# Edge pieces in three buffers of two steps in a GNN-and-MoE kernel on one core

## The chip, the cores and the metric

The kernel runs on one NeuronCore of one Trainium2 chip. The metric is device time in microseconds, from the first to the last instruction of one launch and what the launch adds. The names of the engines are those of the profile: PE (matrix multiply, with PEld for its weight loads), DVE (vector), ACT (scalar, activations), POOL (GpSimd, which issues the indirect transfers) and SP (which issues most plain transfers). Each engine works through its own instructions in order.

## The reference, cut to what matters

There are 6250 nodes with 256 features and 100,000 edges with 96 features, sorted by their target node `dst`. A node needs the sum, the maximum and the mean over its edges; these go with the normalized node features through a two-layer network (1024 hidden units), and the result through a mixture of 16 experts of which two are chosen per node.

```python
out1 = segment_sum(edge_attr, col); cnt = segment_sum(ones, col)
out2 = where(cnt > 0, segment_max(edge_attr, col), 0)
out3 = out1 / maximum(cnt, 1.0)
h = concatenate([x, out1, out2, out3, u[batch]], axis=1)      # x is layer-normed
h = relu(h @ W1 + b1) @ W2 + b2                               # returns h + x
# then, on the layer-normed result: top-2 of 16 experts, relu MLP 256-512-256, layernorm, residual
```

All in float32.

## The kernel before, in words

**Tiles and groups.** The nodes are 50 tiles of P = 125 rows, in 13 groups (`GRP`) of GS = 4 tiles, the first of two; the groups run from the last nodes to the first. Groups 0 and 1 (GW = 2) gather their few edges directly: one indirect transfer brings a window of WE = 20 edges per node (`take_window`), and `cut_window`, `sum_window` and `max_window` reduce it. All other groups get their sums from the edge stream.

**The edge stream** (`steps`, `load_edges`, lines 177 to 323). The first 95,000 edges lie in seven regions of JR = 6, 5, 5, 10, 21, 20 and 28 steps; the regions run from the last edges to the first. A step holds one edge for each of 125 x 8 runs (partitions times RR = 8). From step to step DVE carries a running sum and a running maximum backwards through each run: four operations of 125 x 768 elements per step, L309 and L310 (the carried values, masked where a new node begins) and L312 and L313 (the new edges added and compared). In a region's first step ACT copies instead (L305, L306). The results, `rw`, hold 192 values for each edge and are stored to `rows_d` in DRAM (L322). When a region is done, `chain_runs` carries the values over runs and partitions (over PE, L394 to L420) and POOL stores them to `carry_d` (L430). A node's sums are then gathered from `rows_d` (`take_edges`, L712) and `carry_d` (`take_carry`, L719) and joined on DVE (`join_edges`, L725).

Steps come in pieces of up to JS = 3: `chunks` lists 34 of them. A piece has a tile `raw` (edges loaded) and a tile `rw` (rows to store), each from a pool of two buffers. After a piece's last DVE operation SP issues the load of the piece two further on, then the store of this one; both are issued in two halves (80 and 45 partitions). For region 0 the address of the store comes from a register (`rows_of`, `away`). The buffers of `raw` and `rw` also serve, before the stream starts, for the windows of groups 0 and 1 and for the node ids (`early`).

**The order of the work** is written by hand: `at_slot(T, fn, ...)` puts pieces of a group's work in slots, 12 per group, and within a slot the functions issue instructions to all engines. A cost is kept for DVE: what a slot has left goes to the edge stream (`next(stream)`), which thus lies between the other DVE operations in a fixed order. For a group whose hidden layer begins at slot B:

- `take_x` at B - 20 issues the load of x on SP (L666) into one of three buffers `xt`; `stats_x` at B - 14 and B - 13 reads it on DVE (L676).
- `turn`, `hidden` (L761, ACT L763) and `output` (L769) are the network on PE; `residual` (L774), `root_b` (L783, the store of x1 on SP), `scale_b` and `norm_b` (L797, ACT, at B + 15) follow, then `turn_b` (L806).
- `logits`, `choose` (L821 to L828), `rank` (L834 to L841, which makes `mm` and `M`), `rank_2` (L848 on PE), `place` (L857 to L870) find each row's place at its experts, and `send` (L874, POOL) scatters the rows to `xg_d`.

After the last group the experts run in 57 blocks (`run_block`, L1047 to L1066), and a last part adds their results, normalizes and writes the output (L1383 to L1421).

Of the kernel before, what the change touches and what calls it, by code (L numbers as in the profile page):

```python
# [9 lines left out]
F32 = mybir.dt.float32  # L10
# [9 lines left out]
P = 125  # L20
PA = 80
RR = 8
GW = 2
WE = 20
WB = 5
JR = (6, 5, 5, 10, 21, 20, 28)
GR = (1, 1, 1, 2, 3, 2, 1)
JS = 3
KB = 250
GS = 4  # L30
BT = (1, 2, 2, 3, 4) + 6 * (5,) + (4, 2, 2)
# [3 lines left out]
SLOTS = 12  # L35
SLOT = 4.6
IB = (1, 1, 1, 2, 3, 5)
# [5 lines left out]
def kernel(  # L43
# [45 lines left out]
    assert len(BT) % 2 == 0 and (NS - 1) // 4 - NA // 4 - 1 >= len(BT) // 2 and NA % 4  # L89
    assert NA <= -(-(2 * (N - P * GRP[-2][1]) - NE * (SB - 1)) // SB)  # L90
    assert KR == 32 and HC % 4 == 0 and GS * P <= 512 and NT <= GS * NE and wpack.shape[1] == WROW and D == DC * 128 and GF <= 128 and EF <= 128
    assert WE % (2 * WB) == 0 and WB * EF <= 512 and N0 == 2 and GW == 2 and WE <= RR * JS and P * GRP[GW - 1][0] <= EP * JR[0] <= ER // 2 and all(i == 1 for i in IB[:GW])

    dram = ctx.enter_context(tc.tile_pool(name="dram", bufs=1, space=DRAM))

# [70 lines left out]
    keep = [di_p.tile([P, RR, j], F32, name="keep%d" % c) for c, j in enumerate(JR)]  # L166
    bar = [di_p.tile([P, RR, j], F32, name="bar%d" % c) for c, j in enumerate(JR)]
    kall = di_p.tile([P, len(JR), RR], F32, name="kall")
    rawp = edges.enter_context(tc.tile_pool(name="raw", bufs=2, side="right"))
    chunks = []  # L170
    for c, j in enumerate(JR):
        k = -(-j // JS)
# [4 lines left out]
    def load_edges(i):  # L177
        c, s, n = chunks[i]
        e0, J = REG[c]
        raw = rawp.tile([P, RR, JS, EF], F32, name="raw")  # L180
        src = edge[e0:e0 + EP * J].rearrange("(p r j) f -> p r j f", p=P, j=J)
        for o, i_ in halves(raw[:, :, :n], src[:, :, s:s + n]):
            nc.sync.dma_start(o.rearrange("p r j f -> p r (j f)"), i_.rearrange("p r j f -> p r (j f)"))
        raws[i] = raw

    rwp = edges.enter_context(tc.tile_pool(name="rw", bufs=2, side="right"))
    ix = edges.enter_context(tc.tile_pool(name="ix", bufs=1, side="right"))
    chp = edges.enter_context(tc.tile_pool(name="ch", bufs=1, side="right"))
    banks = ctx.enter_context(ExitStack())
    eps = banks.enter_context(tc.tile_pool(name="eps", bufs=1, space=PSUM))  # L190

# [5 lines left out]
    gtp = mlp.enter_context(tc.tile_pool(name="gt", bufs=2))  # L197
    sm = mlp.enter_context(tc.tile_pool(name="sm", bufs=2))
    xrp = mlp.enter_context(tc.tile_pool(name="xr", bufs=1))
    pTp = banks.enter_context(tc.tile_pool(name="pT", bufs=1, space=PSUM))  # L200
    accp = banks.enter_context(tc.tile_pool(name="acc", bufs=5, space=PSUM))
    pGp = banks.enter_context(tc.tile_pool(name="pG", bufs=1, space=PSUM))
# [5 lines left out]
    nf = ix.tile([P, 1], F32, name="nf")  # L208
    misfit = ix.tile([1, 1], I32, name="misfit")
    shift = ix.tile([1, 1], I32, name="shift")  # L210
    early = rwp.tile([P, RR, JS, 2 * EF], F32, name="rw").rearrange("p r j f -> p (r j f)")
    L100 = E // 100
    ids100 = early[:100, 0:L100 + WE].bitcast(I32)
    viol = early[:100, L100 + WE:3 * L100 + WE].rearrange("p (h k) -> p h k", h=2)
# [77 lines left out]
    def steps():  # L292

        for i, (c, s, n) in enumerate(chunks):
            e0, J = REG[c]
            if s + n == J:
                mark_runs(c)
                yield 1.5, False, None
            raw, prev = raws.pop(i), prevs.pop(c, None)
            rw = rwp.tile([P, RR, JS, 2 * EF], F32, name="rw")  # L300
            bcast = [P, RR, EF]
            for j in reversed(range(n)):
                x_j, su, mx = raw[:, :, j, :], rw[:, :, j, 0:EF], rw[:, :, j, EF:]
                if prev is None:
                    nc.scalar.copy(su, x_j)  # L305
                    nc.scalar.copy(mx, x_j)  # L306
                    prev = x_j, x_j
                else:
                    nc.vector.tensor_tensor(su, prev[0], keep[c][:, :, s + j, None].to_broadcast(bcast), op=OP.mult)  # L309
                    nc.vector.tensor_tensor(mx, prev[1], bar[c][:, :, s + j, None].to_broadcast(bcast), op=OP.min)  # L310
                    yield 1.9, False, None
                    nc.vector.tensor_tensor(su, su, x_j, op=OP.add)  # L312
                    nc.vector.tensor_tensor(mx, mx, x_j, op=OP.max)  # L313
                    prev = su, mx
                    if j:
                        yield 1.9, True, None
            prevs[c] = prev
            if i + 2 < len(chunks):
                load_edges(i + 2)
            to = rows_of(c).rearrange("(p r j) f -> p r j f", p=P, j=J)  # L320
            for o, i_ in halves(to[:, :, s:s + n], rw[:, :, :n]):
                nc.sync.dma_start(o.rearrange("p r j f -> p r (j f)"), i_.rearrange("p r j f -> p r (j f)"))  # L322
            yield 1.9, True, c if s == 0 else None
# [224 lines left out]
    def take_window(g, i, w):  # L548
        j = GRP[g][0] - W0 + i
        nc.gpsimd.indirect_dma_start(out=w.rearrange("p k f -> p (k f)"), out_offset=None, in_=flat,  # L550
                                     in_offset=IndirectOffsetOnAxis(ap=win_i[:, j:j + 1], axis=0))
        G[g].setdefault("win", []).append(w)
# [525 lines left out]
    def at_slot(T, fn, *a, cost=0.0):  # L1078
        tasks.append((T, len(tasks), fn, a, cost))
# [21 lines left out]
    for g, (a, z) in enumerate(GRP):  # L1101
        B, n = SLOTS * g, z - a
        if g:
            if g > 1:
                at_slot(max(0, B - 20), take_x, g)
                at_slot(B - 14, stats_x, g, 0, cost=1.2)
                at_slot(B - 13, stats_x, g, 1, cost=1.2)
            if g > 1:
                at_slot(B - 11, root_x, g)
                at_slot(B - 10, scale_x, g, cost=0.5)  # L1110
            at_slot(B - 9, norm_x, g)
            for i in range(n):
                if g >= GW:
                    late = 3 if g == GW else 0
                    at_slot(B - 10 + late + i // 2, take_edges, region[g], g, i)
                    at_slot(B - 9 + late + i // 2, take_carry, region[g], g, i)
                else:
                    for h in range(2):
                        at_slot(2 * i + h, cut_window, g, i, h * WE // 2, (h + 1) * WE // 2, None)
                        at_slot(2 * i + 1 + h, sum_half, g, i, h)  # L1120
                    at_slot(2 * i + 1, max_window, g, i, cost=4.7)
                    at_slot(2 * i + 2, add_window, g, i, cost=0.9)
                    at_slot(2 * i + 2, mask_window, g, i, cost=0.4)
                    at_slot(min(2 * i + 5, SLOTS - 2), mean_window, g, i)
            at_slot(B - 7, keep_x, g)
            for k in range(DC):
                at_slot(B - 6 + k, turn, g, k)
            for i in range(n if g >= GW else 0):
                at_slot(B - (4 if g == GW else 6) + i // 2, join_edges, g, i, cost=0.6)
                at_slot(B - (4 if g == GW else 5) + i // 2, mask_edges, g, i)  # L1130
            for k in range(DC, KC + 1):
                at_slot(B - 3 + k - DC + (1 if g == GW and k < DC + 2 else 0), turn, g, k)
        for i in range(n):
            at_slot(B + HC + 1 + i, residual, g, i, cost=1.1)
        early = GS - n
        at_slot(B + SLOTS + 1 - early, root_b, g)
        at_slot(B + SLOTS + 2 - early, scale_b, g, cost=0.3)
        at_slot(B + SLOTS + 3, norm_b, g)
        for k in range(DC):
            at_slot(B + SLOTS + 4 + k, turn_b, g, k)  # L1140
        at_slot(B + SLOTS + 6, logits, g)
        at_slot(B + SLOTS + 7, choose, g, cost=2.2)
        at_slot(B + SLOTS + 8, rank, g, cost=1.3)
        at_slot(B + SLOTS + 9, rank_2, g)
        at_slot(B + SLOTS + 10, place, g, cost=1.5)
        for i in range(n):
            at_slot(B + SLOTS + 11 + i // 2, send, g, i)
# [38 lines left out]
                                fill[:, None, :].to_broadcast([128, NE, DR]))  # L1186

    at_slot(4, fill_rows)

    def loads_1():  # L1190
        take_x(0)
# [21 lines left out]
        nc.vector.tensor_add(c1, ps_u, b1c)  # L1213

    def windows_of(t, n):
        t = t.rearrange("p r j f -> p (r j f)")
        return [t[:, h * WE * EF:(h + 1) * WE * EF].rearrange("p (k f) -> p k f", f=EF) for h in range(n)]

    a, z = GRP[0]
# [1 line left out]
    base.append(chp.tile([P, RR, 2 * EF], F32, name="ct").rearrange("p r f -> p (r f)")[:, 0:(NT - W0) * 2 * EF]  # L1221
                .rearrange("p (t f) -> p t f", f=2 * EF))
    w1u = wk.tile([P, GS, D], F32, name="xn", bufs=1).rearrange("p i d -> p (i d)")[:GF, 0:HID]
    cut_x = windows_of(xrp.tile([P, GS, 2, DR], F32, name="xr"), 1)[0]
    cut_w = w2s[:P].rearrange("p k d -> p (k d)")[:, 0:WE * EF].rearrange("p (k f) -> p k f", f=EF)
    with tc.manual_schedule():
        load_all_ids()
# [60 lines left out]
    with tc.manual_schedule():  # L1288
# [4 lines left out]
        bounds(0)  # L1293
        index_windows(0)
        for i in range(z - a):
            take_window(0, i, windows_of(rawp.tile([P, RR, JS, EF], F32, name="raw"), 1)[0])
        root_x(0)
        counts(0)
        for t in reversed(range(a1, z1)):
# [3 lines left out]
        bounds(1)  # L1303
        index_windows(1)
        for h in range(2):
            for w in windows_of(rwp.tile([P, RR, JS, 2 * EF], F32, name="rw"), 2):
                take_window(1, len(G[1].get("win", [])), w)
        stats_x(1, 0)
        stats_x(1, 1)
# [20 lines left out]
        for k in range(DC, KC + 1):  # L1330
            turn(0, k)
        cuts += [cut_x]
        for i in range(2):
            load_edges(i)
        for c in range(1, len(JR)):
            load_ids(c)
# [137 lines left out]
```

## Time and profile before

| | us |
|---|---|
| median of 3 runs (lowest, highest) | 1442.02 (1439.64, 1451.39) |
| the profiled execution, its own time | 1443.29 |
| its span, first to last instruction | 1441.3 |
| PE busy | 1193.9 |
| DVE busy | 892.9 |
| ACT busy | 511.2 |
| POOL busy | 530.9 |
| DMA traffic over the span | 292.27 MB, mean 203 GB/s |

Busy time is the time in which an engine executes; the rest of the span it waits. Where the profile names a releaser of a wait, that is what came last by its semaphores. The stages of the execution: set-up and windows until about 125 us, edge stream beside groups until about 790 us, the last groups and the experts until about 1350 us, the last part until the end. PE's clock is granted by a throttle; 1.00 is full speed, and in this profile it is either 1.00 or 0.50. The DMA share is the mean busy share of the core's 16 DMA engines.

### The profile page before, as it was taken

How to read it: one execution, taken by the hardware profiler on the slowest of the kernel's cores; microseconds unless marked ns; L12 is line 12 of the kernel's file. 1: busy time of each engine (PE TensorE's matmuls, PEld its weight loads, DVE VectorE, ACT ScalarE, POOL GpSimd, SP SyncE). 2: the span in 40 equal slices, each digit the busy share in tenths (PEclk: the TensorE clock that was granted, in tenths of full speed). 3: DMA queues.
4: the chain of work that ended last, by engine and by line, in shares of the span. 5: the costliest groups of instructions: out<-in, count | busy, mean ns of one | idle time of the engine just before them, and what ended most of it. 6: DMA issues, size and time to landing. Idle time of an engine off the chain costs nothing. (4 is left out here: it accounts for less than half of the span.)

```text
span 1441.3 us, 16536 instructions
## 1 busy us (share of the span) xinstructions
PE 1193.9 (83%) x4835; PEld 833.1 (58%) x4835; DVE 892.9 (62%) x2319; ACT 511.2 (35%) x1178; POOL 530.9 (37%) x611
## 2 busy tenths in 40 slices
PE   2687377979668779898788999898999999999673
PEld 1353243645435354654455566787888888888562
DVE  5477587969766979878677332344444445444277
ACT  3484135554327353353324432321122212212133
POOL 4123043554574645354251622334333233233100
PEclk9898688989888989999898999999999999999897
DMA  5954758796778996986877323656677887666296
GB/s 167 202 150 125 202 144 229 205 244 184 217 186 239 253 256 173 272 226 179 239 213 225 87 79 102 198 174 230 214 245 248 273 266 240 214 228 226 88 273 195
DMA packets 156309, 292.27 MB, mean 203 GB/s; under 512 B 31379, under 2 KB 95652, under 8 KB 148910
## 3 DMA queue, kind: packets, MB, share of 16 engines
q1 hardware_dynamic: 119870, 234.35, 55.1%
q0 software_dynamic: 36224, 56.33, 13.7%
q8 instruction: 41, 0.67, 0.2%
q14 instruction: 62, 0.51, 0.1%
q10 hardware_dynamic: 112, 0.41, 0.1%
HBM read 169.70 MB, written 123.21 MB: 203 GB/s over the span
## 5 line engine op out<-in xcount | busy, mean ns | idle before, releaser
L761 PE MATMUL acc<-inT,w1x 128*128 128x500 f32 (+1 forms) x832 | 374.2, 600 | 0.0
L761 PEld LDWEIGHTS acc<-inT,w1x 128*128 128x128 f32 x832 | 162.6, 203 | 179.4 <-issue 177.3
L1066 POOL DMA_INDIRECT y_d<-yb,to_i x114 | 134.2, 1178 | 292.5 <-ACT yb L1065 269.8
L1047 PE MATMUL acc<-xT,wt 128*128 128x256 f32 x912 | 221.2, 385 | 7.8 <-ACT hb L1053 6.2
L1060 PE MATMUL acc<-wt,hb 128*128 128x256 f32 x912 | 207.8, 380 | 7.0 <-DVE hb L1051 7.0
L874 POOL DMA_INDIRECT xg_d<-xr,pos_i x100 | 130.0, 1300 | 224.0 <-DVE xr L870 144.0
L769 PE MATMUL acc<-w2s,hT 128*125 128x256 f32 x800 | 190.0, 395 | 11.5 <-ACT hT L763 11.5
L1060 PEld LDWEIGHTS acc<-wt,hb 128*128 128x128 f32 x912 | 172.5, 190 | 32.9 <-DVE hb L1051 9.4
L1047 PEld LDWEIGHTS acc<-xT,wt 128*128 128x128 f32 x912 | 168.1, 190 | 39.2 <-ACT hb L1053 15.7
L769 PEld LDWEIGHTS acc<-w2s,hT 128*125 128x125 f32 x800 | 155.2, 198 | 36.5 <-ACT hT L763 11.9
L1065 ACT ACTIVATE yb<-yb,xb 128x256 f32<-128x256 f32 x114 | 51.7, 500 | 347.5 <-issue 294.3
L763 ACT ACTIVATE hT<-acc,c 128x500 f32<-128x500 f32 (+1 forms) x104 | 68.4, 658 | 208.5 <-PE acc L761 206.3
L1063 DVE TENSOR_TENSOR yb<-acc,xb 128x512 f32<-128x512 f32 x57 | 39.4, 691 | 163.1 <-PE acc L1060 163.1
L309 DVE TENSOR_TENSOR rw<-rw,keep 125x768 f32<-125x768 f32 x81 | 76.8, 948 | 85.1 <-DMA rows_d<-rw 78.0
L485 POOL DMA_INDIRECT gb<-in_dst_dram,blk_i x50 | 69.2, 1383 | 115.8 <-DVE blk_i L482 54.2
L312 DVE TENSOR_TENSOR rw<-rw,raw 125x768 f32<-125x768 f32 x88 | 85.7, 973 | 0.0
L1027 DVE COPY xT<-pT 128x512 f32<-128x512 f32 x57 | 39.3, 690 | 74.3 <-PE pT L1025 74.1
L313 DVE TENSOR_TENSOR rw<-rw,raw 125x768 f32<-125x768 f32 x88 | 83.7, 951 | 0.0
L719 POOL DMA_INDIRECT cg<-carry_d,next_i x44 | 70.2, 1595 | 36.4 <-DMA carry_d<-ct 18.0
L310 DVE TENSOR_TENSOR rw<-rw,bar 125x768 f32<-125x768 f32 x81 | 79.5, 981 | 0.0
L712 POOL DMA_INDIRECT at<-rows_d,first_i x44 | 60.5, 1374 | 34.6 <-PE acc L761 13.6
L806 PE MATMUL pT<-ident,xr 125*128 125x125 f32 x100 | 23.3, 320 | 53.8 <-ACT xr L797 44.6
(294 smaller groups left out, 1525.4 us busy)
## 6 DMA issues: line engine op xcount, KB each, us to landing
wt<-in_wpack_dram SPq DMA_DIRECT2D x57, 1026.0 KB
rows_d<-rw SPq DMA_DIRECT2D x27, 1440.0 KB
rows_d<-rw SPq DMA_DIRECT2D x27, 810.0 KB
raw<-in_edge_dram SPq DMA_DIRECT2D x27, 720.0 KB
xb<-xg_d SPq DMA_DIRECT2D x57, 258.0 KB
raw<-in_edge_dram SPq DMA_DIRECT2D x27, 405.0 KB
eb<-in_eb_dram SPq DMA_DIRECT2D x57, 128.0 KB
rows_d<-rw SPq DMA_DIRECT2D x7, 960.0 KB
```

Of the source, the lines that this page charges most:

```text
L309: nc.vector.tensor_tensor(su, prev[0], keep[c][:, :, s + j, None].to_broadcast(bcast), op=OP.mult)
L310: nc.vector.tensor_tensor(mx, prev[1], bar[c][:, :, s + j, None].to_broadcast(bcast), op=OP.min)
L312: nc.vector.tensor_tensor(su, su, x_j, op=OP.add)
L313: nc.vector.tensor_tensor(mx, mx, x_j, op=OP.max)
L485: nc.gpsimd.indirect_dma_start(out=gbs_[t], out_offset=None, in_=dst_b, in_offset=IndirectOffsetOnAxis(ap=blk_i[:, t:t + 1], axis=0))
L719: nc.gpsimd.indirect_dma_start(out=cg, out_offset=None, in_=carry_d[0:EP * (c + 1), :], in_offset=IndirectOffsetOnAxis(ap=next_i[:, t:t + ...
L761: nc.tensor.matmul(pH[:, :n * P], w1x[:, k, ms], inT[:, k, :n * P], start=False, stop=(k == KC - 1))
L769: nc.tensor.matmul(pO, G[g]["hT"][m][:, i * P:(i + 1) * P], w2s[:, m, :], start=(m == 0), stop=(m == HC - 1))
L874: d = nc.gpsimd.indirect_dma_start(out=xg_d[:, :], out_offset=IndirectOffsetOnAxis(ap=G[g]["pos"][:, i, k:k + 1], axis=0), in_=G[g]["xr"][ ...
L1047: nc.tensor.matmul(pB[i][:, half, :], wt[:, k * FF + m * 128:k * FF + (m + 1) * 128], xT[:, k, :], start=(k == 0), stop=(k == DC - 1))
L1060: nc.tensor.matmul(pY[:, h, :], hb[:, m, h * 128:(h + 1) * 128], wt[:, W2O + m * D:W2O + (m + 1) * D], start=(m == order[0]), stop=(m == o ...
L1066: d = nc.gpsimd.indirect_dma_start(out=y_d[:, :], out_offset=IndirectOffsetOnAxis(ap=BL[b]["to"][:, h:h + 1], axis=0), in_=yb[:, h, :], in ...
```

## The change

Pieces have at most two steps instead of three (`JS`), and `raw` and `rw` have three buffers each instead of two (`JB`); the load issued after a piece is that of the third piece on. The memory of `raw` and `rw` stays as it was (six steps each). Since a buffer of two steps is too small for a window pair, the windows and the node ids get pools of their own, `win0` and `win1`, which are closed before `raw` and `rw` are opened: `open_raw` just before the first loads, `open_rows` in slot 9. `raw` moves to the other side of the memory. And `take_x` of a group is three slots later, at B - 17. The order of the instructions on PE, DVE, ACT and POOL stays the same; on SP there are 49 pieces with four transfers each instead of 34, and the loads of x stand later among them.

```diff
-JS = 3
+JS = 2
+JB = 3
...
-    rawp = edges.enter_context(tc.tile_pool(name="raw", bufs=2, side="right"))
...
-        raw = rawp.tile([P, RR, JS, EF], F32, name="raw")
+        raw = EP_["raw"].tile([P, RR, JS, EF], F32, name="raw")
...
-    rwp = edges.enter_context(tc.tile_pool(name="rw", bufs=2, side="right"))
...
+    win1 = ExitStack()
+    w1p = win1.enter_context(tc.tile_pool(name="win1", bufs=2, side="right"))
...
+    win0 = ExitStack()
+    w0p = win0.enter_context(tc.tile_pool(name="win0", bufs=2))
+    EP_ = {}
+
+    def open_raw():
+        win0.close()
+        EP_["raw"] = edges.enter_context(tc.tile_pool(name="raw", bufs=JB))
+
+    def open_rows():
+        win1.close()
+        EP_["rw"] = edges.enter_context(tc.tile_pool(name="rw", bufs=JB, side="right"))
...
-    early = rwp.tile([P, RR, JS, 2 * EF], F32, name="rw").rearrange("p r j f -> p (r j f)")
+    early = w1p.tile([P, 2 * WE * EF], F32, name="w1")
...
-            rw = rwp.tile([P, RR, JS, 2 * EF], F32, name="rw")
+            rw = EP_["rw"].tile([P, RR, JS, 2 * EF], F32, name="rw")
...
-            if i + 2 < len(chunks):
-                load_edges(i + 2)
+            if i + JB < len(chunks):
+                load_edges(i + JB)
...
-                at_slot(max(0, B - 20), take_x, g)
+                at_slot(max(0, B - 17), take_x, g)
...
+    at_slot(SLOTS * (GW - 1) - 3, open_rows)
...
-            take_window(0, i, windows_of(rawp.tile([P, RR, JS, EF], F32, name="raw"), 1)[0])
+            take_window(0, i, windows_of(w0p.tile([P, WE * EF], F32, name="w0"), 1)[0])
...
-            for w in windows_of(rwp.tile([P, RR, JS, 2 * EF], F32, name="rw"), 2):
+            for w in windows_of(w1p.tile([P, 2 * WE * EF], F32, name="w1"), 2):
...
-        for i in range(2):
+        open_raw()
+        for i in range(JB):
             load_edges(i)
```

More of the change, by code (lines that the diff above doesn't have):

```diff
@@ L91 @@
     assert KR == 32 and HC % 4 == 0 and GS * P <= 512 and NT <= GS * NE and wpack.shape[1] == WROW and D == DC * 128 and GF <= 128 and EF <= 128
-    assert WE % (2 * WB) == 0 and WB * EF <= 512 and N0 == 2 and GW == 2 and WE <= RR * JS and P * GRP[GW - 1][0] <= EP * JR[0] <= ER // 2 and all(i == 1 for i in IB[:GW])
+    assert WE % (2 * WB) == 0 and WB * EF <= 512 and N0 == 2 and GW == 2 and P * GRP[GW - 1][0] <= EP * JR[0] <= ER // 2 and all(i == 1 for i in IB[:GW])
     dram = ctx.enter_context(tc.tile_pool(name="dram", bufs=1, space=DRAM))
@@ L1215, in windows_of @@
     def windows_of(t, n):
-        t = t.rearrange("p r j f -> p (r j f)")
         return [t[:, h * WE * EF:(h + 1) * WE * EF].rearrange("p (k f) -> p k f", f=EF) for h in range(n)]
@@ L1223 @@
     w1u = wk.tile([P, GS, D], F32, name="xn", bufs=1).rearrange("p i d -> p (i d)")[:GF, 0:HID]
-    cut_x = windows_of(xrp.tile([P, GS, 2, DR], F32, name="xr"), 1)[0]
+    cut_x = windows_of(xrp.tile([P, GS, 2, DR], F32, name="xr").rearrange("p i k d -> p (i k d)"), 1)[0]
     cut_w = w2s[:P].rearrange("p k d -> p (k d)")[:, 0:WE * EF].rearrange("p (k f) -> p k f", f=EF)
```

## The prediction, made before the changed kernel was run

> **What bounds the kernel now.** I read the page first, then the waits, then the timelines of DVE and PE side by side.
>
> The page's head, busy line, slices and two of its groups and issues:
>
> ```profile
> span 1441.3 us, 16536 instructions
> PE 1193.9 (83%) x4835; PEld 833.1 (58%) x4835; DVE 892.9 (62%) x2319; ACT 511.2 (35%) x1178; POOL 530.9 (37%) x611
> ...
> PE   2687377979668779898788999898999999999673
> ...
> DVE  5477587969766979878677332344444445444277
> ...
> PEclk9898688989888989999898999999999999999897
> DMA  5954758796778996986877323656677887666296
> ...
> L309 DVE TENSOR_TENSOR rw<-rw,keep 125x768 f32<-125x768 f32 x81 | 76.8, 948 | 85.1 <-DMA rows_d<-rw 78.0
> ...
> rows_d<-rw SPq DMA_DIRECT2D x27, 1440.0 KB
> ```
>
> From slice 23 on (793 us) PE is at 8 or 9 and its clock full: the expert part is PE's own. Before that PE and the clock fall again and again while DVE and the DMA engines are at 6 to 9. This is the edge part (125 to 790 us), and only there can the change act. L309, the first DVE operation of an edge step, waits for the store of the rows.
>
> The waits, total, times and longest:
>
> ```profile
> DVE rw L309 <- DMA rows_d<-rw: 86.8, 12, 10.9
> ...
> PE pg L848 <- DVE mm L839: 36.5, 7, 11.9
> ...
> PE ps L420 <- DVE st L411: 18.6, 2, 14.2
> ...
> ACT rw L305 <- DMA rows_d<-rw: 13.1, 1, 13.1
> ```
>
> How a wait reaches PE is seen in one place, DVE's timeline and then PE's:
>
> ```profile
> 646.27 0.96 DVE L309 TENSOR_TENSOR rw<-rw,keep 125x768 f32<-125x768 f32 x1 [7.00 <-DMA rows_d<-rw]
> ...
> 654.69 0.22 DVE L839 TENSOR_TENSOR mm<-mk 125x64 f32<-125x64 f32 x1
> ```
>
> ```profile
> 654.97 0.68 PE L848 MATMUL pg<-mm,before 125*125 125x64 f32 x2 [6.25 <-DVE mm L839]
> ```
>
> DVE executes in order, so 7.00 us without a free `rw` buffer make `choose` and `rank` late, and PE stands still 6.25 us for `mm`. Stretches around it (busy PE, PEld, DVE, ACT, POOL, then PE's clock, DMA share, GB/s):
>
> ```profile
> 400.00:405.00 5.00, 4.33 (x18) 1.88 (x17) 4.78 (x14) 1.19 (x3) 3.43 (x3) 1.00 0.13 35
> ...
> 640.00:648.70 8.70, 8.70 (x40) 6.71 (x38) 2.43 (x3) 1.96 (x2) 0.00 (x0) 1.00 1.01 246
> 648.70:654.90 6.20, 0.02 (x1) 0.00 (x0) 5.96 (x25) 3.18 (x10) 0.00 (x0) 0.82 0.85 291
> 654.90:659.40 4.50, 4.43 (x14) 3.79 (x15) 4.29 (x12) 2.02 (x6) 0.00 (x0) 0.50 0.12 46
> ```
>
> After the stall PE runs 4.5 us at clock 0.50, which costs about half of that once more. The store queue is full at 640 and idle at 400 and 655: the transfers come in bursts, and the wait is one for a queue, not for mean bandwidth.
>
> **What could be won at most.** In the two timelines nine stalls of PE follow a wait for the rows. Stall and wait, us: 14.2 after 8.8 (end of the stall at 161 us), 11.5 after 7.2 (186), 2.4 after 11.0 (461), 3.2 after 4.0 (596), 6.3 after 7.0 (655), 3.1 after 7.3 (690), 7.1 after 9.5 (722), 4.4 after 8.2 (758), 4.5 after 8.0 (788). The smaller of each pair, summed: 47.0 us. After each, the stretch at clock 0.50 goes on for 3.2, 5.5, 3.4, 5.9, 4.4, 6.9, 5.7, 6.8 and 4.9 us of PE's work, 46.7 in all; half of it, 23.4 us, is lost time. Together 70 us.
>
> **Buffers of two steps.** DVE's operations on edges stay the same and in the same order. What moves is when a buffer must be free. Now the first step of a piece needs the store of the piece before the last: between its issue and its use lie 3 steps of DVE. Afterwards a piece needs the store of the third last, and 4 steps lie between. One step is four operations of about 0.95 us issued 0.87 apart (646.27 to 649.75): 3.5 us. That is the least by which each wait shrinks. With the twelve waits of L309 (8.8, 7.2, 3.2, 10.5, 11.0, 2.3, 4.0, 7.0, 7.3, 9.5, 8.2, 8.0), 3.5 off each leaves 46 of 87. The most is the time that the full queue needs for a step's bytes: a load of 375 KB and a store of 750 KB, 1.15 MB. From 663.6 to 687.0 us the queue took 3.3 MB (a load and a store of three steps), 142 GB/s beside the gathers and scatters of POOL; a step is 8 us there, and 8 off each leaves 8 of 87. So 47% to 91% goes; I take 65%, nearer the low end because the bursts follow each other (429 and 451; 687 and 704) and a wait that is saved comes back in part at the next. 65% of 70 us: 46 us won.
>
> **More and smaller transfers.** Pieces go from 34 to 49, SP's transfers for them from 136 to 196. An issue takes 0.87 to 0.93 us (median of L183 and L322), so 54 us more on SP, which stands waiting for over 600 us; covered by those waits. On the DMA engines the runs get shorter: loads from 1152 to 768 bytes, stores from 2304 to 1536. The packet records show 84, 52, 117 and 79 ns for these. Before: 27,000 x 84 + 7,000 x 52 + 27,000 x 117 + 7,000 x 79 ns over 16 engines, 396 us. After: 46,000 x (52 + 79) plus 3,000 single steps at 29 (the nearest row, 512 bytes) and 52, 392 us. Nothing lost. The Trainium skill ("DMA: Bandwidth & Descriptors", "Rules for kernel authors") speaks against it: transfers should be of 1 MiB or more. With the fixed 2 us that its "Anatomy of one DMA" gives, 60 more transfers would be 120 us if each came alone, by estimate; they overlap here, except in region 0.
>
> **Region 0.** Its rows are stored to a run-time address, and each half waits for the half before: issued at 137.7, 148.0, 156.1 and 164.7 us, the next at 175.7, 38 us in all. Now there are six halves of two thirds the bytes: 38 us if bytes count, 57 if each takes 9.5. The first pair is free sooner in both cases, and it alone decides the wait of 8.8; that stays in the sum.
>
> **x three slots later.** `take_x` moves behind one or two pieces in SP's queue; no longer does SP stand for `norm_b` or for the old x1 store there:
>
> ```profile
> SPq L666 <- DMA x_d<-xt: 31.9, 6, 19.8
> ...
> SPq L666 <- ACT xr L797: 17.1, 2, 15.2
> ```
>
> I count nothing for that: the pieces behind mostly wait for DVE anyway (L183 for L313, 166.8 us). The price is that `stats_x` may come too early. From issue to `stats_x` it is now 29 to 37 us (nine groups from 240 us on); three slots are 16.4 (65.7 us from one `norm_b` to the next, 12 slots), which leaves 13 to 21. The loads landed 8.4 to 21.7 us after issue. Pair by pair the lateness adds up to 20 us; if all landed in 8.4, as in a quiet stretch, nothing. The new place is nearer the quiet stretch: I take 10 us on DVE. A DVE wait costs PE 70/87 of itself by the sum above: 8 us back.
>
> **Closing the window pools early** adds waits only for gathers read before 104 us, while edge work starts at 125: nothing; if that cover were gone, the 16 us of the first raw loads.
>
> **Denser transfers.** The DMA share between 120 and 800 us averages 0.76; 46 us less makes it 0.81. Other stalls that hang on landings (PE for `xr`, 8.9 to 12.8 us at 300, 433 and 510) may grow. Between 0 and 16 us; I take 8.
>
> **Sum:** 46 - 8 - 8 = 30 us off the profiled execution's 1443.3 (span 1441.3 and 2.0 around it), 1413. It lies 1.3 above the median of 1442.0; so 1412 for the median.
>
> **The rivals.**
> - *All of it.* The waits go, x is in time: 70 less 12 for denser transfers, 1385. For it: the lulls at 400, 465 and 540 us (DMA share 0.12 to 0.19) have room. Against: stores landed up to 22.7 us after issue, over six steps.
> - *The queue is the limit, or the third buffer does not work.* SP's transfers share eight completion semaphores, so a store may wait for the one two pieces back (SP waited for `rows_d` at L322 25.4 us in 4 waits already), and a full queue gives a deeper lead nothing. The waits keep their sum; 0 to 10 us won, 1438. For it: DMA share 0.97 to 1.07 within bursts. Against: the same lulls.
> - *x is late* (the other side). `stats_x` in DVE's order holds back what comes behind it, residuals and edge steps. If every load took the longest 21.7 us, it is 5.9 us late on average, 59 over ten groups, times 70/87 is 48 on PE. With the waits for rows shrunk only by 47% (33 us) and 8 for density, 48 - 25 = 23 slower, 1466. It decides from 3.1 us per group on (25 / 10 / 0.8). For it: six of nine loads took over 15 us. Against: they were queued in the busiest part.
>
> **How the numbers follow.** Forecast 0.45, all of it 0.17, no lead 0.20, x late 0.18. About 1% (14 us) is what a measurement of this kernel tells from no change. Faster by more: 0.42 of the forecast, 0.17, and 0.03 of no lead, 0.62. Within: 0.03 and 0.17, 0.20. Slower: 0.18. The range goes from below the full gain, 1380, to inside the late x, 1458.
>
> **What the profile after would show.** L309's wait for `rows_d` down from 86.8 to about 30 us, no PE stall above 8 us at 161 and 186, `stats_x` waiting for x at most 10 us in all, fewer 0.50 stretches before the experts, raw and rows transfers of 960 and 480 KB in 49 pieces, and the unbroken busy part of PE beginning at about 760 instead of 793 us, as long as before. Wrong it is if L309 keeps 70 us or more, or if `stats_x` or an `xr` wait takes over what L309 loses.

## The result, and the profile after

The changed kernel takes 1398.62 us (median of 4 runs, 1398.23 to 1403.48) against 1440.83 us before (median of 4 runs on the same chip). The ratio is 0.9707, with a 95% interval of 0.9668 to 0.9746: 42 us, or 2.9%, faster. The forecast was 1412 us, in a range of 1380 to 1458. The profiled execution after took 1403.48 us, the longest of the four; its span is 1401.7 us.

The lines of the page after that answer to those shown of before. L309, L310, L312, L313 and L322 are now L323, L324, L326, L327 and L336; nearly all other lines of the edge part are 14 further down.

```profile
span 1401.7 us, 16643 instructions
...
PE 1195.1 (85%) x4835; PEld 833.7 (59%) x4835; DVE 898.2 (64%) x2319; ACT 510.6 (36%) x1178; POOL 519.4 (37%) x611
...
PE   2598458979869789998898998899999999999683
...
PEclk9898779989989899999999999999999999999897
DMA  6953687796979897898985143457667786766396
...
L323 DVE TENSOR_TENSOR rw<-rw,keep 125x768 f32<-125x768 f32 x81 | 76.9, 949 | 46.5 <-DMA rows_d<-rw 46.5
...
rows_d<-rw SPq DMA_DIRECT2D x46, 960.0 KB
```

The engines' busy times are nearly what they were: PE's 1.2 us more, POOL's 11.5 us less. So the 39.6 us by which the span is shorter are time in which PE stood still: 1441.3 - 1193.9 = 247.4 us before, 1401.7 - 1195.1 = 206.6 us now. The notches in PE's slices between the 7th and the 22nd are fewer and shallower. L323's wait for the store of the rows is 46.5 us where L309 had 78.0 in this group.

The same for the edge part alone, each with the window up to where PE's unbroken part starts (us of the window, busy time of PE, PEld, DVE, ACT, POOL with instructions, then PE's clock, DMA share, GB/s); first before, then after:

```profile
120.00:792.00 672.00, 530.61 (x1897) 313.61 (x1896) 527.23 (x1346) 279.23 (x607) 298.41 (x268) 0.88 0.77 213
```

```profile
120.00:752.00 632.00, 530.10 (x1911) 312.44 (x1910) 534.83 (x1358) 279.97 (x610) 288.49 (x269) 0.90 0.82 226
```

The same work of PE (530 us) lies in 632 instead of 672 us, and the DMA engines carry 226 GB/s instead of 213. What follows takes 649.3 us before and 649.7 after: the whole gain is made in the edge part.

The waits after (engine, what waits, for what: total, times, longest):

```profile
DVE rw L323 <- DMA rows_d<-rw: 46.5, 8, 13.3
...
PE pT L820 <- ACT xr L811: 29.2, 12, 12.8
...
PE pg L862 <- DVE mm L853: 12.7, 5, 4.1
...
PE ps L434 <- DVE st L425: 11.5, 2, 8.7
...
DVE bsa L690 <- DMA xt<-in_x_dram: 7.7, 7, 2.8
...
ACT rw L319 <- DMA rows_d<-rw: 7.6, 1, 7.6
```

Of before, the second of these was not shown yet:

```profile
PE pT L806 <- ACT xr L797: 44.6, 27, 12.8
```

PE's waits for `mm` fell from 36.5 to 12.7 us, those for `xr` from 44.6 to 29.2, those at the chain of runs (L434, before L420) from 18.6 to 11.5. New are 7.7 us in which `stats_x` waits for x.

### The profile page after: what moved, and what is told of

It is laid out like the page before. It is cut to its first block, busy times and chain, and to the rows that moved or that the text cites. A ratio compares the mean times of both kernels' runs of the same rounds, so it can differ in the third digit from the quotient of the medians.

```text
span 1401.7 us, 16643 instructions
## 1 busy us (share of the span) xinstructions
PE 1195.1 (85%) x4835; PEld 833.7 (59%) x4835; DVE 898.2 (64%) x2319; ACT 510.6 (36%) x1178; POOL 519.4 (37%) x611
## 5 line engine op out<-in xcount | busy, mean ns | idle before, releaser
L775 PE MATMUL acc<-inT,w1x 128*128 128x500 f32 (+1 forms) x832 | 378.7, 606 | 0.0
L1080 POOL DMA_INDIRECT y_d<-yb,to_i x114 | 133.1, 1168 | 296.6 <-ACT yb L1079 272.9
L1061 PEld LDWEIGHTS acc<-xT,wt 128*128 128x128 f32 x912 | 169.4, 191 | 39.8 <-ACT hb L1067 15.5
L323 DVE TENSOR_TENSOR rw<-rw,keep 125x768 f32<-125x768 f32 x81 | 76.9, 949 | 46.5 <-DMA rows_d<-rw 46.5
L324 DVE TENSOR_TENSOR rw<-rw,bar 125x768 f32<-125x768 f32 x81 | 84.7, 1046 | 0.0
L327 DVE TENSOR_TENSOR rw<-rw,raw 125x768 f32<-125x768 f32 x88 | 83.8, 952 | 0.0
L326 DVE TENSOR_TENSOR rw<-rw,raw 125x768 f32<-125x768 f32 x88 | 83.6, 950 | 0.0
L726 POOL DMA_INDIRECT at<-rows_d,first_i x44 | 64.4, 1464 | 35.0 <-issue 25.4
L760 ACT COPY inT<-pT 128x500 f32<-128x500 f32 (+1 forms) x65 | 35.9, 552 | 88.5 <-PE pT L759 81.7
L1408 PE MATMUL py<-yk,ident 125*125 125x256 f32 x200 | 52.2, 419 | 18.4 <-DMA yk<-y_d 18.1
```

What stands on the lines that cost most here:

```text
L775: nc.tensor.matmul(pH[:, :n * P], w1x[:, k, ms], inT[:, k, :n * P], start=False, stop=(k == KC - 1))
L1061: nc.tensor.matmul(pB[i][:, half, :], wt[:, k * FF + m * 128:k * FF + (m + 1) * 128], xT[:, k, :], start=(k == 0), stop=(k == DC - 1))
L1080: d = nc.gpsimd.indirect_dma_start(out=y_d[:, :], out_offset=IndirectOffsetOnAxis(ap=BL[b]["to"][:, h:h + 1], axis=0), in_=yb[:, h, :], in ...
```

## The experiments

The lead theory was the forecast's: the gain comes from the third buffer, which lets a store land during four steps of DVE instead of three. Rivals were that x, three slots later, or the pools that close early do it, or the mere size of the pieces. Kernels that were measured together ran on one chip beside the kernel before; each ratio is to that kernel as measured there. Between such sets ratios are compared rather than times.

**The parts alone.** Three kernels separate the parts.

The kernel before with x three slots later, and nothing else:

```diff
-                at_slot(max(0, B - 20), take_x, g)
+                at_slot(max(0, B - 17), take_x, g)
```

> The kernel before with only the load of x three slots later. Theory (the gain comes from the longer lead of the rows' buffers): 0 to 10 us faster than before, L309's wait for the rows' stores stays above 70 us of its 86.8. Rival (the gain comes from x leaving the busy part of the transfers, and from SP no longer standing for it): 25 us or more faster, L309's wait near the 46.5 us of the changed kernel.

Measured: 1443.0 us, ratio 1.001 [0.9974, 1.0045]; L309 waits 79.5 us, `stats_x` 11.3 us for x. x alone brings nothing.

The changed kernel with x back at B - 20 (the same edit the other way round):

> The changed kernel with x at its old slot. Theory: 0 to 10 us slower than the changed kernel, so 1399 to 1409, the wait for the rows' stores 45 to 60 us, no wait of stats_x for x (6 us in the changed kernel). Rival (x is the cause): 1425 or more, the wait back above 75 us.

Measured: 1402.12 us, ratio 0.973 [0.9694, 0.9767]; L323 waits 50.9 us for the rows. The gain is there without x. The interval overlaps that of the whole change, so what x does beside the buffers lies below what these runs resolve. Its profile shows a trade: with x at B - 17 PE waits 8.8 us for `xt` (2.7 with x at B - 20), but 12.7 us for `mm` (17.3).

The pools alone: two buffers of three steps as before and x at B - 20, with the pools of the windows as changed.

```diff
-JS = 2
-JB = 3
+JS = 3
+JB = 2
...
-                at_slot(max(0, B - 17), take_x, g)
+                at_slot(max(0, B - 20), take_x, g)
```

> The changed kernel's pools for the windows, closed in time, but pieces of three steps in two buffers and x at its old slot. Theory: within 5 us of the kernel before, since the windows are read long before the edge stream begins. Rival (the stream starts earlier because its buffers are free earlier): 10 us or more faster, with the gain before 200 us of the span.

Measured: 1443.5 us, ratio 1.0014 [0.9986, 1.0042]. The pools bring nothing. L323 waits 97.9 us here, L309 86.8 in the kernel before and 79.5 in the run with x alone, at the same time within 1 us: so far does the sum of this wait scatter between profiles of kernels that are equally fast.

**Size or number.** Two buffers of two steps, x at B - 17: the pieces shrink, and the lead shrinks with them.

```diff
-JB = 3
+JB = 2
```

> The changed kernel with two buffers of two steps: small pieces, but between the issue of a store and the use of its buffer lie 2 steps instead of 4 (3 in the kernel before). Theory of the lead: slower than before, 1455 to 1500, L309's wait above 110 us. Rival (smaller transfers land sooner, the number of buffers matters little): faster than before, about 1420, the wait below 87 us.

Measured: 1451.56 us, ratio 1.0073 [1.0035, 1.011].

```profile
DVE rw L323 <- DMA rows_d<-rw: 129.3, 21, 14.8
...
PE pg L862 <- DVE mm L853: 51.1, 7, 10.4
...
PE pT L820 <- ACT xr L811: 31.0, 18, 10.9
```

The wait for the rows rises by 42 us over before and PE's wait for `mm` by 15, as the lead of two steps demands. But the kernel is only some 8 to 10 us slower, less than the 11 us or more that the theory of the lead had for it (1455 to 1500). PE's wait for `xr` is near that of the changed kernel (29.2), with two buffers only. Small pieces without the third buffer lose; yet they seem to have a side of their own that gains (more on it behind the experiments).

**Which of the two pools.** First three buffers for `rw` and two for `raw`:

```diff
-        EP_["raw"] = edges.enter_context(tc.tile_pool(name="raw", bufs=JB))
+        EP_["raw"] = edges.enter_context(tc.tile_pool(name="raw", bufs=2))
...
-            if i + JB < len(chunks):
-                load_edges(i + JB)
+            if i + 2 < len(chunks):
+                load_edges(i + 2)
...
-        for i in range(JB):
+        for i in range(2):
```

> The changed kernel, but only rw has three buffers of two steps; raw has two, and the load after a piece is that of the second piece on. Theory (the lead of the rows' stores is what counts): most of the gain stays, 1400 to 1415, L309's counterpart waits about 50 us for stores; a raw load has two steps to land, which took 9.8 us on average, so some waits for raw appear. Rival (the third load in flight counts as much): 1425 or more, with waits for raw above 40 us.

Measured: 1402.2 us, ratio 0.9723 [0.969, 0.9757].

```profile
DVE rw L326 <- DMA raw<-in_edge_dram: 43.3, 11, 9.5
...
DVE rw L323 <- DMA rows_d<-rw: 12.0, 6, 4.3
```

The gain is all there with two buffers of `raw`. The wait for the rows has all but gone, and in its place DVE waits for the edges' load: 43.3 + 12.0 = 55.3 us together, somewhat more than the 46.5 and 50.9 us for the rows alone in the changed kernel and the one with x back. I read the wait that remains as one for SP's transfers as a whole, of which now one and now the other ends it; no run shows that by itself.

Then two for `rw` and three for `raw`:

```diff
-        EP_["rw"] = edges.enter_context(tc.tile_pool(name="rw", bufs=JB, side="right"))
+        EP_["rw"] = edges.enter_context(tc.tile_pool(name="rw", bufs=2, side="right"))
```

> The changed kernel, but only raw has three buffers of two steps, rw has two. Theory: no gain is left, 1445 to 1460 like two of two (1451.6), waits for stores above 110 us. Rival (loads count): 1415 or less.

Measured: 1454.66 us, ratio 1.0095 [1.0068, 1.0123].

```profile
DVE rw L323 <- DMA rows_d<-rw: 125.5, 18, 14.8
...
PE pg L862 <- DVE mm L853: 56.8, 7, 11.2
```

Without the third buffer of `rw` the gain is gone. The two runs together show where the change works: in the one more buffer of rows. At two steps a piece it is worth more than the whole change, some 50 to 56 us (ratios of 1.0073 and 1.0095 with two, 0.9723 and 0.9707 with three). No run has four steps of lead with three-step pieces, or three with two-step ones, so how lead and size share the 42 us is open.

**A third step of the same kind.** Six buffers of one step; the lead becomes five steps in the same memory.

```diff
-JS = 2
-JB = 3
+JS = 1
+JB = 6
```

> The changed kernel with pieces of one step in six buffers of the same memory: five steps between the issue of a store and the use of its buffer instead of four, runs of 384 and 768 bytes, 380 transfers for the stream. Theory of the lead: the wait for stores falls again, to 25 us or less, and the time to 1385 to 1398. Rival (a store waits for the one two pieces back, since SP's transfers share eight completion semaphores; or short runs are slow): the wait stays at 45 us or more and the time rises above 1410, with SP waiting longer for stores than its 21 us.

Measured: 1445.45 us, ratio 1.0012 [0.9985, 1.0038], so no faster than before. The wait for the rows fell to 13.4 us as the lead theory wants, and against the rival; the time is the rival's. But `stats_x` waited 46.0 us for x, DVE 49.7 us for `cg`, and in the stretch from 120 to 280 us PE was busy for only 104.7 us (118.3 in the changed kernel). Two causes were to be told apart, what the one-step pieces do to region 0 and to x, and what they cost by themselves. Three more runs did this.

**Region 0.** The changed kernel with the rows of region 0 at a fixed address; this leaves out the shift that this address takes for other inputs.

```diff
-        if c:
-            return rows_d[r0:r0 + n, :]
+        return rows_d[r0:r0 + n, :]
```

> The changed kernel with region 0's rows stored to a fixed address; left out is the shift of that address which the other branch of the kernel needs for inputs that do not fit the regions. So its six half stores no longer wait for each other. Theory (the stalls of PE before 190 us, 8.7 and 12.9 us, come from these waits): both shrink to a few us, 10 to 18 us faster than the changed kernel, 1381 to 1389. Rival (region 0 is bounded by the transfers of that time, 0.86 of the engines, or by the chain over runs): within 4 us of it.

Measured: 1385.61 us, ratio 0.9623 [0.9597, 0.965]. That is 13 us below the changed kernel. Is it the address, or the order that a run-time address forces on the stores? The next kernel keeps the address and takes away the order between the half stores of region 0, which each have rows of their own; the stores of other regions still wait for them. It also moves loads: in region 0 each half load now stands just before a half store, where both stood before the pair.

```diff
-    def load_edges(i):
+    def load_edges(i, half=None):
...
+        for h, (o, i_) in enumerate(halves(raw[:, :, :n], src[:, :, s:s + n])):
+            if half is not None and h != half:
+                continue
...
-            if i + JB < len(chunks):
...
+            if c and i + JB < len(chunks):
                 load_edges(i + JB)
...
+            for h, (o, i_) in enumerate(halves(to[:, :, s:s + n], rw[:, :, :n])):
+                if not c:
+                    load_edges(i + JB, h)
+                d = nc.sync.dma_start(o.rearrange("p r j f -> p r (j f)"), i_.rearrange("p r j f -> p r (j f)"))
+                if not c:
+                    tc.declare_no_dep(d.ins, group="store", reason="each piece has rows of its own")
+                    tc.add_to_no_dep_group("store", d.ins)
...
```

> The changed kernel, with the address of region 0's rows as it was, but with its six half stores no longer ordered against each other (each half has rows of its own); in region 0 the two half loads stand between the two half stores. Theory (in region 0 each half store waits for the one before it to land, 8 to 11 us each, because its address is known only at run time; with that order gone region 0 is as with the fixed address, 1385.6): 1380 to 1392 us, ratio 0.957 to 0.967, PE's two stalls of 8.7 and 12.9 us at 157 and 184 us fall to some 5 and 6. Rival (what the fixed address brought was the saved read of the address into a register, or another move of SP's queue, not the order): 1395 to 1403, the two stalls above 8 us.

Measured: 1383.22 us, ratio 0.9592 [0.9558, 0.9626], as with the fixed address (the intervals overlap): it is the order, not the address. That the moved loads add nothing is seen in the run with the fixed address, which gains nearly the same without them. This is the fastest kernel of the study, 4.1% below before. PE's timeline at region 0, of the changed kernel and then of this one (start, duration, line, operation, in brackets the stall before it and its releaser):

```profile
157.13 0.70 PE L434 MATMUL ps<-ident,st 96*125 96x96 f32 x2 [8.68 <-DVE st L425]
...
184.73 6.83 PE L783 MATMUL acc<-w2s,hT 128*125 128x256 f32 x18 [12.88 <-ACT hT L777]
```

```profile
152.53 0.71 PE L441 MATMUL ps<-ident,st 96*125 96x96 f32 x2 [5.26 <-DVE st L432]
...
172.11 5.59 PE L790 MATMUL acc<-w2s,hT 128*125 128x256 f32 x18 [5.00 <-ACT hT L784]
```

In the changed kernel the six half stores are issued from 139.1 us on and the first of region 1 at 179.6; here from 135.8 on and the first of region 1 at 162.0. 14 us of the chain are gone, and PE is 12.6 us further at the second stall.

The same in the kernel before, with its two buffers of three steps:

> The kernel before (two buffers of three steps, x at its old slot), with region 0's four half stores no longer ordered against each other, as in the run that took 16 us off the changed kernel. Theory (the chain of six halves cost the changed kernel what it brought back in part: with three buffers the chain of six is longer than that of four, so the order costs the kernel before less): 1430 to 1437 us, and the third buffer alone would be worth 47 to 54 us. Rival (the order costs both the same, some 16 us): 1423 to 1429. Second rival (with two buffers the rows wait on the buffers, not on the order): 1438 to 1446, no change. PE's stall before L420 at 161 us (14.2 us) tells: below 8 us by the theory and the first rival, above 11 by the second.

Measured: 1435.81 us, ratio 0.9937 [0.9909, 0.9965]. So the order cost the kernel before 8 us or so, and the changed kernel 15 to 17. The time lies where my theory put it, but the reason that I gave does not hold: the chain of six halves was hardly longer than that of four (40.5 us from the first store to the first of region 1, against 38.1 before). Here too the chain shrinks to 26 us and both stalls of PE with it (9.6 and 5.1 us; the first stays above the 8 us that the theory had as its sign), 10.9 us less in the two, and L311 still waits 74.8 us for the rows. Free of the order, the buffers are worth some 50 us instead of 42 (ratios of 0.9937 and 0.9592). That the kernel before gains less because some of the time won in region 0 is lost at later waits for want of a third buffer is my reading; no run shows it by itself.

**One step again, without its two handicaps.** Six buffers of one step, region 0 without the order, x at B - 20.

> Six buffers of one step (same six steps of room), x at its old slot, and region 0's half stores no longer ordered against each other. The first run with one step (1445.5) had twelve such stores in a chain and x 46 us late. Theory A (those two made its loss; the lead in steps sets the rest): 1375 to 1395 us, rows wait under 15, no wait of stats_x for x. Rival B (pieces of one step cost by themselves: twice the transfers, runs of half the length, and the queue or the semaphores hold them up): 1410 to 1445, with cg and raw waits of 40 us and more and a DMA share that stays at 0.81 at 213 GB/s.

Measured: 1409.49 us, ratio 0.978 [0.9738, 0.9822]. The two handicaps were worth some 35 us (1445.5 to 1409.5), so the theory explains the larger part. But some 26 us are missing to the kernel with two-step pieces (1383.2), in the rival's direction; its lower bound of 1410 is met within 1 us. The rows wait 26.2 us where the theory had less than 15, so neither theory has it alone. The page's rows on the queue that carries SP's plain transfers (packets, MB, and the time of the packets as a share of 16 engines' span), of the changed kernel and then of this one:

```profile
q1 hardware_dynamic: 150800, 234.36, 56.5%
```

```profile
q1 hardware_dynamic: 245652, 234.37, 58.1%
```

The same bytes take 0.565 x 1401.7 = 792 us of all 16 engines in the changed kernel, 0.551 x 1441.3 = 794 before, and 0.581 x 1406.9 = 817 here. From three steps to two the shorter runs cost nothing, from two to one 25 us of DMA time per engine. DVE's `join_edges` waits 47.3 us for `cg` (in the run without the order at two steps 16.0 for `cg` and 13.7 for `at`), and PE 41.7 us for `mm` (11.4). That the 25 us of DMA time are what makes these waits is likely but was not tried by itself.

**The price of a late x.** The changed kernel with x two more slots later:

```diff
-                at_slot(max(0, B - 17), take_x, g)
+                at_slot(max(0, B - 15), take_x, g)
```

> The changed kernel with x two slots later still (some 14 us). The forecast priced DVE's waits for x at 0.8 us of the span for each us. If that holds: stats_x waits about 6 to 14 us more in each of some ten groups, 50 to 100 us in all, and the time is 1430 to 1470 us. Rival (DVE's own slack and the planner cover it, as 7.7 us of waits cost nothing so far): waits of 40 us and more and a time within 6 us of the changed kernel's 1398 to 1403.

Measured: 1462.96 us, ratio 1.0147 [1.0109, 1.0185].

```profile
DVE bsa L690 <- DMA xt<-in_x_dram: 78.1, 8, 20.2
PE acc L770 <- DVE xt L788: 74.5, 8, 15.7
```

The forecast's price holds: 70.4 us more of DVE's waits than in the changed kernel make its profiled span 57.7 us longer (1459.4 against 1401.7), 0.82 us for each; between the medians it is 64.3 us, 0.91 us for each. Both are net figures, since DVE's wait for the rows fell by 20.2 us at the same time. The rival, that slack covers it, is out. DVE's order carries the wait on through `residual` (L788) to PE almost in full. Two slots turn a gain of 42 us into a loss of 21.

## Why the prediction was right, and where its steps were not

The sign, the cause and the range held: the third buffer shortens the wait for the rows, and x only just comes in time. The size was some 10 us short (30 us forecast on the profiled execution, 39.8 measured; 42 between the medians), and it came that near only because terms were off in both directions. The terms of the sum against PE's waits and busy time in the two profiles, and, because single profiles scatter, against the means of three profiles with two buffers of three steps (before, x alone, pools alone) and three with the third buffer (changed, x back, two of `raw`); gains are positive:

| term, us | forecast | the profiled pair | means of three |
|---|---|---|---|
| stalls after waits for the rows (PE for `mm` and `st`) | 30.6 | 30.9 | 23.8 |
| half clock (PE busy) | 15.2 | -1.2 | 8.4 |
| x late (PE for `xt`) | -8 | -7.5 | |
| denser transfers (PE for `xr`) | -8 | 15.4 | 11.3 |
| no term (PE for `gT`) | 0 | 7.8 | 6.5 |
| all, by the span | 30 | 39.6 | 42.2 |

In the third column the first row is 36.5 - 12.7 and 18.6 - 11.5, the fourth 44.6 - 29.2; the means are 33.2 to 15.5 for `mm`, 17.8 to 11.6 for `st`, 42.1 to 30.8 for `xr`, 8.2 to 1.7 for `gT`, and 1197.7 to 1189.3 for PE's busy time. The rest, small waits of both signs, is left out. For x no mean stands, since x lies elsewhere in some of the six.

- *The wait for the rows* was to shrink by 47% to 91%, with 65% taken. It shrank by 46% in the profiled pair (86.8 to 46.5), just below the low end; the choice of 65% was not right. About 30 us were named as the sign; 46.5 it is. (The 3.3 MB in the working of the upper end should be 3.5, three times 1.15; the 8 us for a step stay.)
- *PE's stalls behind it* came out at 30.9 against 30.6 us in the pair, but the match is luck. The largest stall of PE for `mm` before, 11.94 us at 389.55, was not among the forecast's nine: it follows a wait of DVE for `cg` (8.68 us at 377.82), not for the rows, and it gave 7.9 of the 30.9 us. Of the nine, the one for `hT` did not shrink (11.54 to 12.88), and two, at 690 and 758, are stalls for `xr` and stand in the fourth row. Taken as the forecast listed them, the nine fell from 56.7 us (47.0 as the forecast counted them) to some 30. Nor does each wait of DVE reach PE: the longest that is left, 13.28 us at 430, has no stall of PE above 2 us behind it before 473.
- *The half clock* was to give 15 us (65% of 23.4). The stretches at 0.50 did become fewer (from 100 to 800 us the clock was at 0.50 for 170.7 us before and 133.1 after), but some of that time PE stands still anyway. PE's busy time shows nothing in the pair and 8.4 us in the means: the term was about twice too large.
- *Denser transfers* were to cost 8 us, through longer waits for `xr`. This is the step that failed, and in its sign. The DMA share rose to 0.82 as foreseen (0.81), but none of the three stalls named grew by more than 0.2 us: 9.25, 12.76 and 8.85 us before, 9.44, 12.78 and 4.92 after. Up to 7.5 us more of the 15.4 come from the two stalls at 690 and 758. That smaller pieces let POOL's transfers land sooner had been overlooked; the paragraph behind this list shows it. I had priced the pieces by their bytes and their number, not by what stands behind them.
- *More and smaller transfers cost nothing:* right for two steps (794 to 792 us of DMA time), and the 54 us of issues on SP are nowhere seen. The rule of the Trainium skill ("DMA: Bandwidth & Descriptors", "Rules for kernel authors") to make transfers 1 MiB or more speaks for the larger halves of 1440 and 810 KB; the changed kernel is faster with 960 and 540, all below it. The 2 us that the prediction took from the Trainium skill (the same page, "Anatomy of one DMA") stand there for transfers issued by GpSimd; these are SP's, and no run here shows such a cost. Only with 480 and 270 KB, at one step, is there a price; the packets' time is 25 us longer there, but that this makes it was not tried.
- *Region 0* was put at 38 to 57 us for the six half stores in a row; 40.5 it was, near what the bytes alone give. But that the first pair "alone decides the wait of 8.8" was wrong: what waits for the first pair shrank (ACT's wait at L305 from 13.1 us to 7.6 at L319), but the second and third pairs then held DVE for 7.49 and 4.17 us (to 164.48 and 179.68). No stall of PE above 8 us was to be left there, and 8.68 and 12.88 were, the second no shorter than before (11.54). The order among the halves was worth some 16 us to the changed kernel, which no rival named.
- *x three slots later* was to make DVE wait 10 us, at 0.8 each. It waits 7.7 us, and the run with x at B - 15 puts the price at 0.82 to 0.91. The rival with x late was right in its mechanism and wrong in its place: the cliff lies between B - 17 and B - 15. SP freed from standing for `norm_b` was counted at nothing, and x alone brought nothing.
- *The pools:* nothing forecast, nothing measured.
- *PE's unbroken part* begins at 752 to 760 us; 760 was forecast.

POOL's transfers land sooner beside smaller pieces. It is plainest at a stall for which the forecast had no term: in the kernel before, ACT waits for a store to `carry_d` to land, and PE then for `gT`, which ACT copies next.

```profile
238.34 0.45 ACT L382 COPY ct<-rw 125x96 f32<-125x96 f32 x2 [9.95 <-DMA carry_d<-ct]
```

```profile
239.88 1.10 PE L806 MATMUL pT<-ident,xr 125*128 125x125 f32 x4 [9.22 <-ACT gT L807]
```

PE's wait for `gT` is 6.5 to 9.2 us in the four kernels with three-step pieces and 0.3 to 2.2 in the eight with two-step ones, those with two buffers of `rw` included. From issue to the last record of its landing a store to `carry_d` took 10.4 to 11.9 us on average in the four and 6.9 to 8.3 in the eight. The waits for `xr` point the same way (36.6 to 45.0 in the four, 24.0 to 33.5 in the eight), less clearly: the 36.6 belong to the one of the four with x at B - 17, where seven of the eight have it or later, so x may have a share in them.

The rival "the queue is the limit" has a part of the truth: with three buffers of rows 46 to 55 us of waits remain, and they move from the stores to the loads when `raw` has two buffers. What it said of a deeper lead, that it gives nothing, was wrong. And its evidence was misread: the 25.4 us that SP waited at L322 are the order in region 0, not shared semaphores.

```profile
SPq L322 <- DMA rows_d<-rw: 25.4, 4, 9.4
```

Its four waits are those of the three later half stores of region 0 and of region 1's first. Without the order the row is gone in the kernel before, and in the one-step kernel with its 190 stores 1.3 us are left of it.

## What to carry to other kernels

With a fixed memory for buffers, count the steps of compute between the issue of a store and the reuse of its buffer: three buffers of two steps give four, two of three give three, and the move was worth 42 us here. Smaller pieces also let POOL's transfers land sooner here, and at one step the DMA time itself grew; look at the packets' time by queue before going further down. Move a load later only after reading how far from its use it lands in the busiest stretch: three slots cost nothing here, and two more cost some 63 us. And where stores go to an address known only at run time, look whether they wait for each other though their places are apart.

## What the runs showed of the hardware that was not expected

The stores to an address known only at run time were ordered one behind the other. In region 0 of the changed kernel the second half of each pair was issued 6.5 us after the first (139.05 and 145.56, 151.79 and 158.24, 164.40 and 170.85), in region 1, with fixed addresses, 0.7 us after it (179.57 and 180.29). Each of the later five, and region 1's first, waits for the half before it to land, six times and 20.8 us in all in the changed kernel (1.6 us in one wait in the run without the order):

```profile
SPq L336 <- DMA rows_d<-rw: 20.8, 6, 5.6
```

And a packet's time went nearly in proportion to its bytes, for each direction by itself, down to the shortest runs. Loads: 384 bytes 26 ns (one-step kernel without the order), 768 bytes 50 ns (changed kernel; of its 49,000 such packets 3,000 are stores), 1152 bytes 84 ns (before). Stores: 768 bytes 45 ns, 1536 bytes 83 ns, 2304 bytes 117 ns in the same three. Averaged over the 16 engines the packets of the edge stream took 395.5 us before, 396.1 in the changed kernel (392 was forecast), and 420.8 with one step: of these last 25 us about 17 come with the stores, whose runs went from 1536 to 768 bytes, and 8 with the loads.
